# A decoder layer on one core: weights' sums two quarters ahead, and the softmax's scaling moved into the exponential

## The chip, the cores and the metric

The kernel runs on one core of one Trainium2 chip. The metric is the device time of one execution in microseconds (us). A core has five engines that matter here, each with an instruction queue of its own: TensorE (PE in the profile; PEld is its loading of stationary operands), VectorE (DVE), ScalarE (ACT), GpSimd (POOL) and SyncE (SP), which only issues transfers here. An engine takes its instructions in order; an instruction that waits for another engine holds everything behind it in its queue.

## The reference

The input `x` has 32 sequences of 64 tokens with 512 features, all float32. The layer has three stages, each added to its input after a layer norm:

```python
q = rmsnorm(x @ Wq + bq, gq); k = rmsnorm(x @ Wk + bk, gk); v = x @ Wv + bv   # 32 heads of 128
attn = softmax(q @ k.T / sqrt(128)) @ v;  x = x + attn @ Wo + bo
x = x + cross_attention(layernorm(x), ctx)
x = x + top8_of_64_router_mix(layernorm(x))
```

Only the first stage is touched. For it two things matter. The norm of a query row is one factor for all its scores, the norm of a key row is one factor for a column of scores. And the softmax is taken over 64 keys for each query.

## The kernel before

**Tiling.** There are 2048 tokens, cut into two halves of two quads each; a quad is four tiles of 128 tokens (8 sequences). Heads are taken two at a time, a head group `hg` of 0 to 15. The products of inputs with Wq, Wk and Wv are made with Strassen's scheme in Winograd's form, with 7 products in the place of 8; for most head groups in two levels, 49 products in the place of 64. The seven transformed inputs of a half (`inner_x`, from `halves_x`) are kept in seven blocks of a pool of 13 blocks (`blocks`, 2048 floats a partition). The weights need sums too. They are made per head group by `WeightSet`: set 0 to 3 belong to the outer products (1, 5), (2, 6), (7, 3) and (4), and each holds the raw or outer-summed parts (`raw`) and four inner sums (`more`).

**Windows and steps.** Group 0 of each half is done with one level, one quad after the other (`single`). Groups 1 to 15 are done in a window of both quads (`double`, `Window`). A window has four quarters, one for each weight set, and a quarter has four steps; (k, m) means step m of quarter k. `Window.outer` gives the order of products: step 0 has products 1 and 5, step 1 has 6 and 2, step 2 has 7 and 3, step 3 has 4 (in quarter 3, with a single outer product: 1 and 2; 6 and 5; 7 and 3; 4). Products 1, 6, 7 and 4 add onto one and the same PSUM bank `pa`; between two of them a copy (`keep`, L779 or L789, and the L792 of `end`) must have read it. Beside the products each step takes a part of the values' products (`Window.v`, at L978 for `ValueGroup`), of which windows of odd `hg` have none left in quarter 3.

**Attention beside the products.** `Line` carries finished units (a head group of a quad) through attention. In a window, `scale` stands at (1,0) and (2,0), `turn` at (1,1) and (3,2), `attend` at (1,3) and, as `end`, at (3,3). `attend` issues, in this order: the scores of one unit (PE), the mix of the unit before with its values (PE), at the end of a window also the inverse roots of the norms (ACT, L725 and L727, by transfer into DRAM and back by `fetch`, L624), the softmax (`probabilities`, L667) and the store of the mixed unit (`store`, four ACT instructions L710 and a transfer).

**The softmax** (L304 to L318) is a generator. Its first part multiplies scores by `gains` (DVE L309), takes the maximum over 64 keys (L310), subtracts it (L311) and takes the exponential (ACT L312). `gains` holds the keys' inverse roots, broadcast over partitions by `fetch`, times the queries' inverse roots `rq`, multiplied in by POOL in `scale` (L646). Its second part, sums (DVE L315), reciprocals (L317) and the product with them (POOL L318), is put into the list `waiting`. `take_waiting` takes one entry from it. In a window that happens twice a step: after the products of the step (L891), and at the end of `v` (L754), after the values' products. So the second part of a softmax issued at (1,3) or (3,3) is issued in the next step 0, behind that step's copies of products 1 and 5 and ahead of the values' work.

**What sets the order.** In the attention stage the order on PE, DVE, ACT and POOL is that of the program (`manual_schedule`, with `plan` and `behind` as the lists of what goes into which step). SP's transfers are placed by the planner.

**Weights.** `load_qk` (L1748) issues a set's loads and `sums_of` with `inner_sums` its sums on POOL: L175 subtracts outer parts (128x512), L199 inner ones (128x256; 128x128 for the fourth set). In a window's quarter k the set k+2 is loaded at step 0, and the set k+1 is summed at steps 1 and 2 (sets 4 and 5 are the next window's 0 and 1). Each set of queries and keys is loaded from both weights; the fourth takes two outer subtractions. Values' sets are loaded and summed at half that pace.

Of the kernel before, what the change touches and what calls it, by code (L numbers as in the profile page):

```python
# [8 lines left out]
F32 = mybir.dt.float32  # L9
# [32 lines left out]
def decoder_layer(  # L42
# [47 lines left out]
    class Weights:  # L90
# [3 lines left out]
        def __init__(self, name, hg, queues, between=None):  # L94

            parts = []
            self.right = {}
            for n, pair in enumerate(((1, 7), (2, 3), (5, 6), (4,))):
                it = block(f"w{n}_{name}")[:, 0 : 4 * W3].rearrange(
                    "p (h c j d) -> p h c j d", h=2, c=2, j=3  # L100
                )
                parts.append(it)
                self.right.update({i: it[:, h] for h, i in enumerate(pair)})
            for k in range(2):
                for j, src in enumerate((wq, wk, wv)):
                    for c in range(2):
                        queues[j].dma_start(
                            out=parts[k][:, :, c, j, :],
                            in_=src[bass.ts(2 * k + c, P), bass.ts(hg, HW)].rearrange(
                                "p (h d) -> p h d", d=HD  # L110
                            ),
                        )
                if between and k == 0:
                    between()
            self.values = {i: it[:, :, 2, :] for i, it in self.right.items()}
# [28 lines left out]
    class WeightSet:  # L144
# [2 lines left out]

        def __init__(self, n, name, sources, width, base):  # L150
            self.n = n
            it = block(f"ws{n}_{name}")
            self.raw = it[:, 0 : 8 * HD].rearrange("p (o c f) -> p o c f", o=2, c=2)
            self.more = it[:, 8 * HD : 16 * HD].rearrange("p (e o d) -> p e o d", e=4, o=2)
            for j, src in enumerate(sources):
                to = self.raw[:, :, :, j * width : (j + 1) * width]
                if n < 2:
                    for c in range(2):
                        nc.sync.dma_start(
                            out=to[:, :, c],  # L160
                            in_=src[bass.ts(2 * n + c, P), base : base + 2 * width].rearrange(
                                "p (o f) -> p o f", o=2
                            ),
                        )
                else:
                    base_ = base + (width if n == 2 else 0)
                    nc.sync.dma_start(
                        out=to.rearrange("p o c f -> p (o c) f"),
                        in_=src[:, base_ : base_ + width].rearrange("(k p) f -> p k f", p=P),
                    )  # L170
            self.slots = slice(1, 2) if n == 3 else slice(0, 2)

        def outer_sums(self, before):
            def subtract(out, a, b):
                nc.gpsimd.tensor_tensor(  # L175
                    *(it.rearrange("p c f -> p (c f)") for it in (out, a, b)), ALU.subtract
                )

            a, b = (self.raw[:, o] for o in range(2))
            if self.n == 0:  # L180
                subtract(b, b, a)
            elif self.n == 1:
                subtract(b, b, before.raw[:, 1])
            elif self.n == 2:
                subtract(a, b, a)
            else:
                subtract(b, b, before.raw[:, 0])
                subtract(b, b, a)

        def inner_sums(self, part):  # L190
            at = self.slots
            b11, b12, b21, b22 = (
                self.raw[:, at, c, j * HD : (j + 1) * HD] for c in range(2) for j in range(2)
            )
            t1, t2, t4, t7 = (self.more[:, e, at, :] for e in range(4))
            for out, a, b in ((t1, b12, b11), (t2, b22, t1), (t4, b21, t2), (t7, b22, b12))[
                2 * part : 2 * part + 2
            ]:
                nc.gpsimd.tensor_tensor(out, a, b, ALU.subtract)  # L199

        def inner(self, s):

            if self.n == 3:
                s = 1
            b11, _, b21, b22 = (
                self.raw[:, s, c, j * HD : (j + 1) * HD] for c in range(2) for j in range(2)
            )
            t1, t2, t4, t7 = (self.more[:, e, s, :] for e in range(4))
            return {1: b11, 2: b21, 3: b22, 4: t4, 5: t1, 6: t2, 7: t7}

    normed = scratch.tile([NT // 2, P, D], F32, tag="normed", name="normed")
# [89 lines left out]
            nc.tensor.transpose(pt[:, j, :], src[:, j, :], ident)  # L301
        return pt

    def softmax(s, gains, prob, name):  # L304


        g, k = s.shape[1], s.shape[2]
        mx = small.tile([P, g], F32, tag="mx", name=f"mx_{name}")
        nc.vector.tensor_tensor(prob, s, gains, ALU.mult)  # L309
        nc.vector.tensor_reduce(mx, prob, AX.X, ALU.max)  # L310
        nc.vector.tensor_tensor(prob, prob, _bc(mx, k), ALU.subtract)  # L311
        nc.scalar.activation(prob, prob, AF.Exp)  # L312
        yield
        sums = small.tile([P, g], F32, tag="sums", name=f"sums_{name}")
        nc.vector.tensor_reduce(sums, prob, AX.X, ALU.add)  # L315
        inv = small.tile([P, g], F32, tag="inv", name=f"inv_{name}")
        nc.vector.reciprocal(inv, sums)  # L317
        nc.gpsimd.tensor_tensor(prob, prob, _bc(inv, k), ALU.mult)  # L318

    quads = {}  # L320
    halves_x = {}
# [118 lines left out]
    class HeadGroup:  # L440
# [7 lines left out]
        def __init__(self, hg, quad, w, kept):  # L448
            self.hg, self.quad, self.w, self.name = hg, quad, w, f"{hg}_{quad}"

            self.qk, self.gains = {}, None
            self.v = {
                (h, ab): kept[:, h, 2 * (hg % 2) + ab, :, :] for h in range(HG) for ab in range(2)
            }
# [169 lines left out]
        def fetch(self):  # L624

            if self.gains is None:
                both = work.tile([P, 2, NQ, P], F32, tag="rsb", name=f"g_{self.name}", bufs=2)
                self.gains = both[:, 0, :, :]  # L630
            self.rq = small.tile([P, NQ * 2], F32, tag="rq", name=f"rq_{self.name}")
            for h in range(HG):
                rows = slice(h * SEQ, (h + 1) * SEQ)
                rq, rk = (self.row[j, h].rearrange("a b p -> (a b p)") for j in range(2))
                nc.sync.dma_start(
                    out=self.gains[rows].rearrange("p i k -> p (i k)"),
                    in_=rk.partition_broadcast(SEQ),
                )
                nc.sync.dma_start(
                    out=self.rq[rows], in_=rq.rearrange("(g n) -> n g", n=SEQ)  # L640
                )

        def scale(self):

            it = self.gains.rearrange("p i (b k) -> p (i b) k", b=2)
            nc.gpsimd.tensor_tensor(it, it, _bc(self.rq, SEQ), ALU.mult)  # L646
            k = self.all[:, :, 1, :]
            nc.scalar.activation(k, k, AF.Copy, scale=gqk)

# [17 lines left out]
        def probabilities(self):  # L667
            self.prob = work.tile([P, NQ, P], F32, tag="prob", name=f"prob_{self.name}", bufs=1)
            it = softmax(
                self.s.rearrange("p i b k -> p (i b) k"),  # L670
                self.gains.rearrange("p i (b k) -> p (i b) k", b=2),
                self.prob.rearrange("p i (b k) -> p (i b) k", b=2),
                self.name,
            )
            next(it)
            waiting.append(lambda: next(it, None))

        def turn_probabilities(self):

# [53 lines left out]
    class Window:  # L733
# [5 lines left out]
        def __init__(self, units, n, half, values):  # L739
# [6 lines left out]
            both = work.tile([P, 2, NQ, P], F32, tag="rsb", name=f"g_{self.name}", bufs=2)  # L746
            for t, unit in enumerate(units):
                unit.row = self.row[t]
                unit.gains = both[:, t, :, :]

        def v(self):
            if self.values:
# [994 lines left out]

    def load_qk(n, k):  # L1748
        hg, half = groups[n]
        qk_sets[n, k] = WeightSet(k, f"q{hg}_{half}", (wq, wk), HD, hg * HW)  # L1750

    def load_v(half, g, k):
        v_sets[half, g, k] = WeightSet(k, f"v{g}_{half}", (wv,), HW, g * 2 * HW)

    def sums_of(sets, *at):

        it = sets[at]
        it.outer_sums(sets.get((*at[:-1], at[-1] - 1)))
        it.inner_sums(0)

    for n, (hg, half) in enumerate(groups):
# [53 lines left out]
        else:  # L1815
# [2 lines left out]
            def also(n, m, it):  # L1818
                more.setdefault((n, m), []).append(it)

            places = [(n, k) for k in range(4)] + [(n + 1, k) for k in range(2)]
            for k in range(4):
                for at in places[k + 2 if (hg, k) != (1, 0) else 1 : k + 3]:
                    if at[0] == n or hg < NHG - 1:
                        also(k, 0, lambda at=at: load_qk(*at))
                at = places[k + 1]
                if at[0] == n or hg < NHG - 1:
                    also(k, 1, lambda at=at: sums_of(qk_sets, *at))
                    also(k, 2, lambda at=at: qk_sets[at].inner_sums(1))
            for k in range(2):  # L1830
                at = (half, hg // 2, 2 * (hg % 2) + k + 1)
                if at[2] == 4:
# [253 lines left out]
```

## Time and profile before

Three runs took 1883.17, 1883.83 and 1885.5 us; the median is 1883.83. The profiled execution took 1886.6 us, its span (first to last instruction) is 1884.9 us, and its granted TensorE clock 0.995.

| of the profiled execution | value |
|---|---|
| PE busy | 1831.8 us, 97% of the span |
| DVE busy | 1298.2 us, 69% |
| POOL busy | 1170.1 us, 62% |
| ACT busy | 664.9 us, 35% |
| two-level products of queries and keys (L768), busy on PE | 731.9 us |
| inner weight sums for them (L199 on POOL) | 337.1 us, 480 instructions |
| exponential of the softmax (L312 on ACT) | 40.4 us, 64 instructions |
| subtraction of the maximum (L311 on DVE) | 58.0 us, 64 instructions |
| scaling of `gains` (L646 on POOL) | 66.6 us, 60 instructions in windows |

How it is read: a group is all instructions of one line, engine and shape, with its busy time, the mean of one in ns, and the idle time of the engine ahead of them. A wait names the engine and line that released the waiting one last. A timeline row has the start in us, the duration, the engine and line, and in brackets the idle time ahead of it; "x4" means four instructions of one kind merged into one row. Two windows, an even and an odd one, take about 83 us together and repeat seven times in each half.

### The profile page before, as it was taken

How to read it: one execution, taken by the hardware profiler on the slowest of the kernel's cores; microseconds unless marked ns; L12 is line 12 of the kernel's file. 1: busy time of each engine (PE TensorE's matmuls, PEld its weight loads, DVE VectorE, ACT ScalarE, POOL GpSimd, SP SyncE). 2: the span in 40 equal slices, each digit the busy share in tenths (PEclk: the TensorE clock that was granted, in tenths of full speed). 3: DMA queues.
4: the chain of work that ended last, by engine and by line, in shares of the span. 5: the costliest groups of instructions: out<-in, count | busy, mean ns of one | idle time of the engine just before them, and what ended most of it. 6: DMA issues, size and time to landing. Idle time of an engine off the chain costs nothing.

```text
span 1884.9 us, 41677 instructions
## 1 busy us (share of the span) xinstructions
PE 1831.8 (97%) x16500; PEld 1569.0 (83%) x16500; DVE 1298.2 (69%) x2270; ACT 664.9 (35%) x1483; POOL 1170.1 (62%) x1414
## 2 busy tenths in 40 slices
PE   8999999999999989999999999999999999999998
PEld 7887888888888878888888888888888778888876
DVE  6667778787868766677877777787876354544465
ACT  3344443443344433434344433443321212211222
POOL 3678787878888775777888787878833121211120
PEclk9999999999999999999999999999999999999999
DMA  3334444444444443334444344444745222132100
GB/s 114 96 104 134 130 123 121 125 130 116 122 114 114 132 117 90 92 103 124 114 113 125 106 121 113 113 114 118 239 145 191 104 92 79 71 115 101 59 26 23
DMA packets 340241, 211.20 MB, mean 112 GB/s; under 512 B 82320, under 2 KB 319440, under 8 KB 335952
## 3 DMA queue, kind: packets, MB, share of 16 engines
q1 hardware_dynamic: 331856, 202.45, 36.6%
q10 hardware_dynamic: 8192, 6.10, 1.0%
q8 instruction: 131, 2.15, 0.5%
q14 instruction: 62, 0.51, 0.1%
HBM read 168.12 MB, written 40.37 MB: 111 GB/s over the span
## 4 chain that ended last, share of the span: by engine, by line
PE 77%; POOL 11%; DVE 9%; issue 3%; DMA 0%; ACT 0%; POOLq 0%; SPq 0%; DVEq 0%; ACTq 0%
PE p_w L768 24%; PE py L1070 21%; PE va L978 6%; POOL ws_q L175 4%; PE vb L978 4%; PE s L658 4%; POOL qk L848 3%; PE ms_w L904 3%; PE o L695 3%; DVE qk L779 3%; POOL ws_q L199 2%; PE pa L528 2%; POOL g_w L646 2%; PE va L473 1%; PE pt_p L301 1%
## 5 line engine op out<-in xcount | busy, mean ns | idle before, releaser
L768 PE MATMUL p_w<-x,ws_q 128*128 128x256 f32 x2940 | 731.9, 386 | 34.2 <-POOL ws_q L199 20.0
L768 PEld LDWEIGHTS p_w<-x,ws_q 128*128 128x128 f32 x2940 | 521.9, 191 | 113.1 <-POOL ws_q L199 31.3
L199 POOL TENSOR_TENSOR ws_q<-ws_q 128x256 f32<-128x256 f32 x480 | 337.1, 712 | 21.0
L437 ACT ACTIVATE sq<-qk 128x512 f32<-128x512 f32 x256 | 157.5, 629 | 362.6 <-POOL qk L848 219.3
L779 DVE TENSOR_TENSOR qk<-p_w,qk 128x512 f32<-128x512 f32 x360 | 210.6, 596 | 83.6 <-PE p_w L768 72.8
L792 DVE TENSOR_TENSOR qk<-p_w,qk 128x512 f32<-128x512 f32 x360 | 224.0, 624 | 57.7 <-PE p_w L768 49.9
L1070 PE MATMUL py<-wo,a 128*128 128x256 f32 x992 | 227.0, 382 | 0.0
L978 PEld LDWEIGHTS va<-ws_v,x 128*128 128x128 f32 x1568 | 209.0, 191 | 21.0 <-DVE v L994 10.0
L978 PE MATMUL va<-ws_v,x 128*128 128x128 f32 x1568 | 212.6, 276 | 4.4 <-DVE v L994 4.4
L1070 PEld LDWEIGHTS py<-wo,a 128*128 128x128 f32 x992 | 183.8, 190 | 33.5 <-issue 9.0
L318 POOL TENSOR_TENSOR prob<-prob,inv 128x512 f32<-128x512 f32 x64 | 72.3, 1129 | 209.0 <-DVE inv L317 143.0
L978 PEld LDWEIGHTS vb<-ws_v,x 128*128 128x128 f32 x1176 | 154.5, 192 | 6.5
L978 PE MATMUL vb<-ws_v,x 128*128 128x128 f32 x1176 | 158.5, 275 | 0.0
L1070 PE MATMUL py<-wo_t,a 128*128 128x256 f32 x672 | 154.9, 381 | 0.0
L199 POOL TENSOR_TENSOR ws_v<-ws_v 128x256 f32<-128x256 f32 (+1 forms) x224 | 147.4, 668 | 8.8
L1201 POOL TENSOR_TENSOR x<-x,p 128x256 f32<-128x256 f32 x42 | 40.7, 991 | 163.8 <-ACT p L1254 72.9
L1070 PEld LDWEIGHTS py<-wo_t,a 128*128 128x128 f32 x672 | 124.7, 190 | 18.9 <-issue 2.4
L175 POOL TENSOR_TENSOR ws_q<-ws_q 128x512 f32<-128x512 f32 x90 | 116.8, 1298 | 2.4
L710 ACT ACTIVATE ot<-o,bvt 128x256 f32<-128x256 f32 x256 | 99.2, 469 | 2.2 <-PE o L695 2.2
L309 DVE TENSOR_TENSOR prob<-s,g_w 128x512 f32<-128x512 f32 x60 | 41.3, 688 | 84.4 <-PE s L658 66.1
L848 POOL TENSOR_TENSOR qk<-qk 128x256 f32<-128x256 f32 x120 | 89.1, 742 | 5.3 <-DVE qk L792 0.6
L312 ACT ACTIVATE prob<-prob 128x512 f32<-128x512 f32 x64 | 40.4, 631 | 135.2 <-DVE prob L311 135.2
(276 smaller groups left out, 2654.9 us busy)
## 6 DMA issues: line engine op xcount, KB each, us to landing
mixed<-ot SPq DMA_DIRECT2D x64, 512.0 KB
a<-mixed SPq DMA_DIRECT2D x32, 1024.0 KB
ws_q<-in_wq_dram SPq DMA_DIRECT2D x120, 128.0 KB
ws_q<-in_wk_dram SPq DMA_DIRECT2D x120, 128.0 KB
ws_q<-in_wq_dram SPq DMA_DIRECT2D x60, 256.0 KB
ws_q<-in_wk_dram SPq DMA_DIRECT2D x60, 256.0 KB
g_w<-row_w SPq DMA_DIRECT2D x120, 128.0 KB
ws_v<-in_wv_dram SPq DMA_DIRECT2D x56, 256.0 KB
```

The costliest lines, as they stand in the source:

```text
L175: nc.gpsimd.tensor_tensor(*(it.rearrange("p c f -> p (c f)") for it in (out, a, b)), ALU.subtract)
L199: nc.gpsimd.tensor_tensor(out, a, b, ALU.subtract)
L318: nc.gpsimd.tensor_tensor(prob, prob, _bc(inv, k), ALU.mult)
L437: nc.scalar.activation(sq, of, AF.Square)
L658: nc.tensor.matmul(s[h * SEQ : (h + 1) * SEQ, i, b, :], qk[:, 0, tok], qk[:, 1, tok], start=True, stop=True,)
L710: nc.scalar.activation(ot[:, h, :, b * SEQ : (b + 1) * SEQ], o[b][:, h, :, :], AF.Identity, bias=bvt[:, hg * HG + h : hg * HG + h + 1],)
L768: nc.tensor.matmul(bank[:, s, :], right[s][i], inner_x[self.half, o][i], start=first and s == 0, stop=True, skip_group_check=True,)
L779: nc.vector.tensor_tensor(to(t, j), bank, add(t, j), ALU.add)
L792: nc.vector.tensor_tensor(to(t, j), bank, to(t, j), ALU.add)
L848: on.tensor_tensor(to, to, what, ALU.add)
L978: nc.tensor.matmul(bank[:, s, bass.ts(t, HD)], x[:, bass.ts(t, HD)], right[s][i], start=first and s == 0 and t == 0, stop=True, skip_group ...
L1070: nc.tensor.matmul(py, a[:, g, :], b[g // KH][:, g % KH, :], start=n == 0 and g == 0, stop=n == last and g == NHG - 1,)
```

## The change

**Softmax.** `gains` becomes `rk`, the keys' inverse roots alone; POOL's multiplication by `rq` goes from `scale`. The maximum is taken over scores times `rk`; a small DVE instruction makes minus the maximum times `rq`, 8 values a partition. The subtraction over 512 columns goes. In the place of one exponential over 512 columns stand eight over 64, one for each of the 8 groups of 64 keys in a partition's row, since scale and bias of an ACT instruction are one value a partition: `rq` is the scale, the small result the bias. Four of them are issued in the first part, then the generator yields; the other four are a second part, and sums, reciprocals and product a third. Two entries go into `waiting` in the place of one.

**Weights' sums.** In quarter k the set k+3 is loaded and the set k+2 is summed, so sums stand two quarters ahead of their products; the first window of a half loads sets 1 to 3 in its first quarter and sums sets 2 and 3 together in its second. Four blocks hold the sets of queries and keys. The fourth set is not loaded: its outer part is the difference of the two outer parts of the second set (`before.raw`), one subtraction. Two of the inner sums (t1 and t7) are made by one instruction of twice the size.

**Layouts.** A set's parts are laid out so that a load's rows are of 256 floats, as they lie in the weights, in place of 128; loads of the two row chunks are joined, those of the third set (and of the values' third and fourth) split by row halves. The one-level weights (`Weights`) are loaded by 6 transfers in place of 12, in the same way.

```diff
-                    "p (h c j d) -> p h c j d", h=2, c=2, j=3
+                    "p (c j h d) -> p c j h d", h=2, c=2, j=3
...
-                self.right.update({i: it[:, h] for h, i in enumerate(pair)})
+                self.right.update({i: it[:, :, :, h, :] for h, i in enumerate(pair)})
...
-                    for c in range(2):
-                        queues[j].dma_start(
-                            out=parts[k][:, :, c, j, :],
...
+                    queues[j].dma_start(
+                        out=parts[k][:, :, j].rearrange("p c h d -> p c (h d)"),
...
-        def __init__(self, n, name, sources, width, base):
-            self.n = n
+        def __init__(self, n, name, sources, base):
+            self.n, self.full = n, n != 3 or len(sources) == 1
             it = block(f"ws{n}_{name}")
...
+            self.slots = slice(1, 2) if n == 3 else slice(0, 2)
+            if not self.full:
+                return
+            width = places[0].shape[-1]
+            for to, src in zip(places, sources):
                 if n < 2:
-                    for c in range(2):
+                    nc.sync.dma_start(
+                        out=to.rearrange("p c o f -> p c (o f)"),
+                        in_=src[bass.ts(n, 2 * P), base : base + 2 * width].rearrange(
+                            "(c p) f -> p c f", p=P
+                        ),
+                    )
+                else:
+                    base_ = base + (width if n == 2 else 0)
+                    for o in range(2):
                         nc.sync.dma_start(
-                            out=to[:, :, c],
...
+                            out=to[:, :, o],
+                            in_=src[bass.ts(o, 2 * P), base_ : base_ + width].rearrange(
...
+            elif self.full:
+                subtract(b, b, before.raw[:, :, :, 0])
+                subtract(b, b, a)
             else:
-                subtract(b, b, before.raw[:, 0])
-                subtract(b, b, a)
+                subtract(b, before.raw[:, :, :, 0], before.raw[:, :, :, 1])
...
-            for out, a, b in ((t1, b12, b11), (t2, b22, t1), (t4, b21, t2), (t7, b22, b12))[
-                2 * part : 2 * part + 2
-            ]:
-                nc.gpsimd.tensor_tensor(out, a, b, ALU.subtract)
+            if part == 0:
+                nc.gpsimd.tensor_tensor(
+                    self.more[:, 0:2, at, :],
+                    self.raw[:, :, 1, at],
+                    self.raw[:, 0, :, at],
+                    ALU.subtract,
+                )
+            else:
+                nc.gpsimd.tensor_tensor(t2, b22, t1, ALU.subtract)
+                nc.gpsimd.tensor_tensor(t4, b21, t2, ALU.subtract)
...
-    def softmax(s, gains, prob, name):
+    def softmax(s, rk, rq, prob, name):
...
-        nc.vector.tensor_tensor(prob, s, gains, ALU.mult)
+        neg = small.tile([P, g], F32, tag="neg8", name=f"neg_{name}")
+        nc.vector.tensor_tensor(prob, s, rk, ALU.mult)
         nc.vector.tensor_reduce(mx, prob, AX.X, ALU.max)
-        nc.vector.tensor_tensor(prob, prob, _bc(mx, k), ALU.subtract)
-        nc.scalar.activation(prob, prob, AF.Exp)
+        nc.vector.scalar_tensor_tensor(neg, mx, -1.0, rq, ALU.mult, ALU.mult)
+
+        def exps(part):
+            for c in range(part * g // 2, (part + 1) * g // 2):
+                at = slice(c, c + 1)
+                nc.scalar.activation(
+                    prob[:, c, :], prob[:, c, :], AF.Exp, bias=neg[:, at], scale=rq[:, at]
+                )
+
+        exps(0)
+        yield
+        exps(1)
         yield
         sums = small.tile([P, g], F32, tag="sums", name=f"sums_{name}")
...
-            it = self.gains.rearrange("p i (b k) -> p (i b) k", b=2)
-            nc.gpsimd.tensor_tensor(it, it, _bc(self.rq, SEQ), ALU.mult)
             k = self.all[:, :, 1, :]
...
-            waiting.append(lambda: next(it, None))
+            waiting.extend([lambda: next(it, None)] * 2)
...
-        it.outer_sums(sets.get((*at[:-1], at[-1] - 1)))
+        before = at[-1] - (1 if it.full else 2)
+        it.outer_sums(sets.get((*at[:-1], before)))
...
-            places = [(n, k) for k in range(4)] + [(n + 1, k) for k in range(2)]
+            places = [(n, k) for k in range(4)] + [(n + 1, k) for k in range(3)]
+            makes = [places[k + 2 : k + 3] for k in range(4)]
+            loads = [places[k + 3 : k + 4] for k in range(4)]
+            if hg == 1:
+                loads[0] = places[1:4]
+                makes[0], makes[1] = places[1:2], places[2:4]
             for k in range(4):
-                for at in places[k + 2 if (hg, k) != (1, 0) else 1 : k + 3]:
+                for at in loads[k]:
                     if at[0] == n or hg < NHG - 1:
                         also(k, 0, lambda at=at: load_qk(*at))
-                at = places[k + 1]
-                if at[0] == n or hg < NHG - 1:
-                    also(k, 1, lambda at=at: sums_of(qk_sets, *at))
-                    also(k, 2, lambda at=at: qk_sets[at].inner_sums(1))
+                for at in makes[k]:
+                    if at[0] == n or hg < NHG - 1:
+                        also(k, 1, lambda at=at: sums_of(qk_sets, *at))
+                        also(k, 2, lambda at=at: qk_sets[at].inner_sums(1))
```

## The prediction

> **What bounds the kernel now.** I read the busy shares first, then who waits for whom, then the timelines of two neighbouring windows, engine by engine, and last the groups by shape for durations.
>
> ```profile
> span 1884.9 us, 41677 instructions
> PE 1831.8 (97%) x16500; PEld 1569.0 (83%) x16500; DVE 1298.2 (69%) x2270; ACT 664.9 (35%) x1483; POOL 1170.1 (62%) x1414
> ...
> PE p_w L768 <- POOL ws_q L199: 20.0, 28, 1.3
> PE p_w L768 <- DVE qk L779: 6.7, 19, 0.6
> ```
>
> TensorE (PE) is busy 97% of the span, so every gain must come out of about 53 us of idle time, and every new wait of PE is paid in full. The largest wait is for GpSimd (POOL) making weight sums: 28 times, always the same two places in 14 of the odd windows. The timeline of PE there (start, duration, group, wait ahead of it), quarter 3 of the window at 648 to 685:
>
> ```profile
> 679.56 1.13 PE L768 MATMUL p_w<-x,ws_q 128*128 128x256 f32 x4
> 680.87 1.13 PE L768 MATMUL p_w<-x,ws_q 128*128 128x256 f32 x4 [0.18 <-POOL ws_q L199]
> 683.25 1.13 PE L768 MATMUL p_w<-x,ws_q 128*128 128x256 f32 x4 [1.25 <-POOL ws_q L199]
> ```
>
> Four of these matmuls take 0.87 us when they follow each other (eight take 1.73 in the chain), so the step at 680.87 starts 0.44 late, and the one at 683.25 starts 1.51 late. Step (3,0) at 679.56 is 0.36 late too (0.87 + 0.44 behind the steps before it), for the outer sum of L175. That is 2.3 us a window, and all of it is the fourth set, whose sums stand only one quarter ahead. Even windows lose 0.2 at (3,0).
>
> Now the place where the softmax sits. Window start at 647.58, the same window: ScalarE (ACT), then VectorE (DVE), then PE.
>
> ```profile
> 649.21 0.63 ACT L312 ACTIVATE prob<-prob 128x512 f32<-128x512 f32 x1 [1.88 <-DVE prob L311]
> 649.74 1.55 ACT L710 ACTIVATE ot<-o,bvt 128x256 f32<-128x256 f32 x4
> 651.17 0.86 ACT L782 ACTIVATE qk<-p_w,bqd 128x256 f32<-128x256 f32 x2
> ```
> ```profile
> 648.05 1.12 DVE L311 TENSOR_TENSOR prob<-prob,mx 128x512 f32<-128x512 f32 x1
> 649.10 0.68 DVE L789 TENSOR_TENSOR qk<-p_w,bqd 128x512 f32<-128x512 f32 x1
> 649.87 0.69 DVE L315 TENSOR_REDUCE sums<-prob 128x8 f32<-128x512 f32 x1
> 650.59 0.20 DVE L317 RECIPROCAL inv<-sums 128x8 f32<-128x8 f32 x1
> 650.71 0.64 DVE L991 TENSOR_TENSOR v<-va,v 128x512 f32<-128x512 f32 x1
> 651.37 0.69 DVE L789 TENSOR_TENSOR qk<-p_w,bqd 128x512 f32<-128x512 f32 x1
> ```
> ```profile
> 652.92 1.89 PE L768 MATMUL p_w<-x,ws_q 128*128 128x256 f32 x8
> ```
>
> To be seen: the row sum L315 starts 0.03 us after the exponential ends (649.84), and DVE works strictly in the order of the program. Behind it stands L789 at 651.37, which reads the bank `pa` after product 6; product 7, PE's group at 652.92, adds onto that bank and may not start before. L789 ends at 652.06, and where PE does wait for such a copy (663.43 behind a copy ending at 663.29) it starts 0.14 after it: 0.72 us of slack here.
>
> **The exponential, now eight.** Before, one instruction of 0.63, whose successor starts 0.53 after it. The prices of the new ones come from these groups (mean ns last before the bar):
>
> ```profile
> L437 ACT ACTIVATE sq<-qk 128x512 f32<-128x512 f32 x256 | 157.5, 629 | 362.6 <-POOL qk L848 219.3 <-DVE qk L792 59.5 <-DVE qk L779 53.1
> L648 ACT ACTIVATE qk<-qk,gqk 128x1024 f32<-128x1024 f32 x64 | 73.8, 1153 | 0.0
> L1424 ACT ACTIVATE ex_f<-lg_f,neg_f 128x64 f32<-128x64 f32 x14 | 4.8, 340 | 21.6 <-DVE neg_f L1421 21.6
> L1662 ACT COPY bqk<-pt_b 128x64 f32<-128x64 f32 x1 | 0.2, 231 | 0.0
> ```
>
> 64 columns with a per-partition bias take 0.34 (L1424), 0.11 over the copy without one (0.231). No row has scale and bias both per partition. Copies from PSUM grow from 0.369 at 256 columns to 0.582 at 512, 0.83 ns a column; by that L437 at 1024 would be 1.055, and L648 with its per-partition scale takes 1.153: 0.10 more. So 0.34 + 0.10 = 0.44, and as successors start about 0.10 before the end (four L710 of 0.469 in 1.55), 0.34 each in a row. Bounds: 0.17 if neither operand cost anything (0.26 less the overlap), 0.43 if nothing overlapped. I take 0.34.
>
> The nearest row has one such operand and stands at 0.24 in a row; by it alone the total would be 1933 (worked out below). The Trainium skill, "ScalarE: Activation LUTs", section "What ACT_TABLE_LOAD costs", gives 186 ns + 0.833 a column, about 93 for each per-partition operand and about 93 of overlap; for 64 columns an estimate of 0.33 in a row, so it speaks against eight short ones, and by it the sum below is some 4 us lower.
>
> **The wait that this makes.** Half of the exponentials are issued in the attend step, then come the four L710, and the other half one list entry later, at the head of the next step, behind its two L782. L315 follows at the second entry. DVE loses L311 and gains a 128x8 instruction (0.20, as L317; at most 0.69 as the reductions). At the window start above: negated maximum 648.05 to 648.25; exponentials from 648.29, 4 x 0.34 to 649.65; L710 1.42 to 651.07; L782 0.73 to 651.80; second half 3 x 0.34 + 0.44 to 653.26. L315 653.30, L317 654.02, L789 654.14 to 654.82, product 7 at 654.96 in place of 652.92: **2.04 us**. The other three places by the same steps:
>
> - Even window start (605.98; negation from 606.45, product 7 before at 611.32): second half ends 611.65, L789 612.53 to 613.21, product 7 at 613.35: 2.03.
> - Even window, attend at (1,3) (negation from 627.66, product 7 before at 632.47, no L782): second half ends 632.14, copy L779 633.02 to 633.70, product 7 at 633.84: 1.37, less the 0.2 at (3,0): 1.17.
> - Odd window, (1,3) (negation from 670.43, product 7 before at 674.73): product 7 at 676.61, 1.88. Then quarter 3. Followed through DVE's queue, which now runs 1.9 late with little idle time in it: L994 680.24, the copy for (3,1) ends 682.65, (3,1) at 682.79, its copy 683.55 to 683.95, (3,2) at 684.09 instead of 683.25. So 0.84 is left: the 2.3 us that POOL gives back are mostly eaten, since the copies of DVE bind almost as early as POOL did (before, the copy ahead of (3,1) ended at 680.71, 0.16 ahead of PE).
>
> Queued behind the wait on DVE are the copies and the value sums; on ACT, L648 and the value copies shift by 1 to 2 us, and the next users are over 2 us later; POOL's L318 comes 2.3 to 3.3 later, and its product is turned a quarter later (620.94 for the softmax at 605).
>
> **The sums two quarters ahead.** A set's sums get a quarter (some 10 us) more lead, so the waits for L199 and L175 go: gains of 2.3 and 0.2, already netted above. POOL loses per window two L646 (1.11 each), one L175 (1.27) of the fourth set, and joins two L199 (0.78 each) into one of 128x512: between 1.27 (L175) and 1.56, I take 1.3. Some 4.5 us of POOL a window, all off the path once PE no longer waits for it. What would be late next are L848's additions at (2,2), which DVE and the squares wait for: odd window, POOL frees L318 at 676.9, L848 to 678.4, sums 2.65, L848 681.0 to 682.6, ahead of the 683.5 where DVE needs them.
>
> **Loads.** SP issues 8 instead of 12 loads a window for queries and keys (2, 2, 4, 0), at 0.4 to 0.5 each, and 2 x 256 KB less for each fourth set; values stay at 6, the first weights go from 12 to 6. They are hidden: a load is issued a quarter ahead of its sum, as before, and now two quarters and more ahead of its use. The ring of four leaves no spare block (7 inputs + 4 + 2 value sets = 13), so a load waits for PE to finish the set three quarters back, as SP does now (199 us for p_w at L167). If that cover failed, the sums would still have a quarter: bounds 0 and the old 2.3 a window; I take 0.
>
> **The sum.** 14 odd windows x (2.04 + 0.84) = 40.3; 14 even x (2.03 + 1.17) = 44.8; the two first windows, without the POOL waits of the others, 2 x (2.04 + 1.88) = 7.8; the second unit of each half's single pair, an estimate of 1 each (between 0 and 2.04): 2; the tail, where PE already waits 0.46 for L318 at 1377.84 and the probabilities come between 1.2 and 2.9 later: 2. Together +97. The profiled execution took 1886.6, 2.8 over the median: 1983.6, or 1981 on the median's scale.
>
> **Rivals.**
> - Cheaper exponentials: each 0.01 less in a row takes 0.08 off each place. At 0.24 the places give 1.24, 0.04, 1.23, 0.37: 14 x 2.88 + 9 = +49, 1933. At 0.17: 0.68, -0.5, 0.67, -0.2: about +14, 1898. At 0.43: +142, 2026. L648 speaks against the first two.
> - Faster: L315 doesn't hold DVE's copies. One mechanism: the row sums of the second half reach DVE's queue behind the copy of product 6, so PE never waits; then only the POOL waits go. Gain between 20.7 (the waits of PE as listed) and 14 x 2.3 + 14 x 0.2 = 35: 1849 to 1863. It decides if the sums are issued at least 2.0 us later in DVE's queue or the eight exponentials cost under 0.08 each. The order L789, L315, L317, L991 in the profile, which is the program's, speaks against it.
> - POOL stays the wait: if the fused sums or the full ring made the sets late again, the 2.3 would stay on top of the rest: 1981 + 14 x 1.5, about 2002. POOL's 4.5 us less speaks against it.
>
> **How the numbers follow.** As forecast, 1960 to 2000: 0.60; cheaper exponentials, 1890 to 1960: 0.22; faster: 0.10; above 2000: 0.06; within 0.2% (what a measurement of this kernel can tell from no change, some 4 us): 0.02. The range, 1898 to 2005, leaves out the faster case and the far end.
>
> **What would show it.** Right: PE's longest waits for p_w turn from POOL L199 to DVE's copies, at steps (0,2) and (2,2), 1 to 2 us each, twice a window; the row sums wait for ACT's exponentials 60 times; no wait for L199. ACT's busy time grows by some 140 us. Wrong: if the exponentials stand 0.2 apart, or DVE takes its copies ahead of the row sums, or PE's order leaves more slack at product 7 than 0.15 to 0.9 us.

## The result and the profile after

The changed kernel takes 2003.55 us (median of 4 runs, 2001.9 to 2007.45) against 1883.96 us for the kernel before on the same chip (4 runs, 1883.17 to 1885.5): a ratio of 1.0637, 95% interval 1.0618 to 1.0655. It is 119.6 us slower; 97 were forecast. The profiled execution has a span of 2002.6 us, 117.7 more than the one before, at a mean granted clock of 0.990.

The head of the page after, with the busy shares:

```profile
span 2002.6 us, 41393 instructions
PE 1853.2 (93%) x16500; PEld 1577.0 (79%) x16500; DVE 1278.3 (64%) x2270; ACT 803.0 (40%) x1931; POOL 1022.9 (51%) x1144
```

The waits of TensorE (PE) after, in us, times, longest:

```profile
PE p_w L791 <- DVE qk L802: 68.5, 100, 2.3
PE p_w L791 <- DVE qk L812: 50.0, 29, 1.9
PE pt_p L314 <- POOL prob L342: 6.3, 2, 3.5
```

GpSimd (POOL) has 147 us less to do, and no wait of PE for a weight sum is left (20.0 us before). In its place PE waits 118.5 us for VectorE's (DVE's) copies of the products (L802 and L812 are L779 and L789 of before). ScalarE (ACT) has 138 us more. The groups that say why; the last number behind the bar is the wait ahead of the group:

```profile
L330 ACT ACTIVATE prob<-prob,neg,rq 128x64 f32<-128x64 f32 x512 | 183.6, 436 | 91.4 <-DVE neg L325 91.4
L339 DVE TENSOR_REDUCE sums<-prob 128x8 f32<-128x512 f32 x64 | 43.9, 686 | 155.1 <-ACT prob L330 155.1
L871 DVE TENSOR_TENSOR qk<-qk 128x256 f32<-128x256 f32 x120 | 101.4, 845 | 0.0
```

The row sums wait 155.1 us for the exponentials, where they waited 1.5. And VectorE's additions of the two quadrants (L871, L848 of before) take 845 ns each; no instruction of theirs was changed. The same group before:

```profile
L848 DVE TENSOR_TENSOR qk<-qk 128x256 f32<-128x256 f32 x120 | 70.5, 587 | 0.0
```

The start of an even window after, on ACT, then on DVE, then PE (the window starts at 645.93, its product 7 at 653.26):

```profile
646.78 1.44 ACT L330 ACTIVATE prob<-prob,neg,rq 128x64 f32<-128x64 f32 x4 [1.12 <-DVE neg L325]
648.12 1.53 ACT L733 ACTIVATE ot<-o,bvt 128x256 f32<-128x256 f32 x4
649.54 0.83 ACT L805 ACTIVATE qk<-p_w,bqd 128x256 f32<-128x256 f32 x2
650.26 1.44 ACT L330 ACTIVATE prob<-prob,neg,rq 128x64 f32<-128x64 f32 x4
```
```profile
651.73 0.69 DVE L339 TENSOR_REDUCE sums<-prob 128x8 f32<-128x512 f32 x1 [3.94 <-ACT prob L330]
652.45 0.20 DVE L341 RECIPROCAL inv<-sums 128x8 f32<-128x8 f32 x1
652.57 0.64 DVE L812 TENSOR_TENSOR qk<-p_w,bqd 128x512 f32<-128x512 f32 x1
```
```profile
653.26 3.32 PE L791 MATMUL p_w<-x,ws_q 128*128 128x256 f32 x8 [1.83 <-DVE qk L812]
```

This is the chain that the prediction drew, link by link: four exponentials of 0.436 each in 1.44 us, the stores, the two biased copies, the other four exponentials, then the row sum with the copy of product 6 behind it, then PE 0.05 us after that copy (0.14 had been put down). DVE stands still for 3.94 us.

### The profile page after: what moved, and what is told of

It is laid out like the page before. It is cut to its first block, busy times and chain, and to the rows that moved or that the text cites. A ratio compares the mean times of both kernels' runs of the same rounds, so it can differ in the third digit from the quotient of the medians.

```text
span 2002.6 us, 41393 instructions
## 1 busy us (share of the span) xinstructions
PE 1853.2 (93%) x16500; PEld 1577.0 (79%) x16500; DVE 1278.3 (64%) x2270; ACT 803.0 (40%) x1931; POOL 1022.9 (51%) x1144
## 4 chain that ended last, share of the span: by engine, by line
PE 60%; DVE 21%; ACT 13%; issue 3%; DMA 1%; POOL 1%; SPq 0%; DVEq 0%; ACTq 0%; POOLq 0%
PE py L1093 19%; PE p_w L791 18%; ACT prob L330 8%; PE va L1001 4%; ACT ot L733 4%; DVE qk L802 4%; PE s L680 3%; PE ms_w L927 3%; DVE sums L339 2%; DVE mx L324 2%; DVE qk L871 2%; DVE prob L323 2%; PE vb L1001 2%; DVE qk L815 2%; DVE v L1017 1%
## 5 line engine op out<-in xcount | busy, mean ns | idle before, releaser
L791 PE MATMUL p_w<-x,ws_q 128*128 128x256 f32 x2940 | 747.2, 391 | 128.3 <-DVE qk L802 68.5
L791 PEld LDWEIGHTS p_w<-x,ws_q 128*128 128x128 f32 x2940 | 527.4, 192 | 220.5 <-DVE qk L802 94.2
L802 DVE TENSOR_TENSOR qk<-p_w,qk 128x512 f32<-128x512 f32 x360 | 210.3, 592 | 84.5 <-PE p_w L791 82.4
L330 ACT ACTIVATE prob<-prob,neg,rq 128x64 f32<-128x64 f32 x512 | 183.6, 436 | 91.4 <-DVE neg L325 91.4
L206 POOL TENSOR_TENSOR ws_q<-ws_q 128x512 f32<-128x512 f32 x120 | 139.2, 1160 | 9.4
L339 DVE TENSOR_REDUCE sums<-prob 128x8 f32<-128x512 f32 x64 | 43.9, 686 | 155.1 <-ACT prob L330 155.1
L186 POOL TENSOR_TENSOR ws_q<-ws_q 128x512 f32<-128x512 f32 x90 | 114.5, 1272 | 2.3 <-PE p_w L791 2.3
L871 DVE TENSOR_TENSOR qk<-qk 128x256 f32<-128x256 f32 x120 | 101.4, 845 | 0.0
```

Of the source, the lines that this page charges most:

```text
L206: nc.gpsimd.tensor_tensor(self.more[:, 0:2, at, :], self.raw[:, :, 1, at], self.raw[:, 0, :, at], ALU.subtract,)
L330: nc.scalar.activation(prob[:, c, :], prob[:, c, :], AF.Exp, bias=neg[:, at], scale=rq[:, at])
L791: nc.tensor.matmul(bank[:, s, :], right[s][i], inner_x[self.half, o][i], start=first and s == 0, stop=True, skip_group_check=True,)
L802: nc.vector.tensor_tensor(to(t, j), bank, add(t, j), ALU.add)
L871: on.tensor_tensor(to, to, what, ALU.add)
```

## Experiments

**Each half of the change alone.** The first kernel is the changed one with the softmax of before; weights' sums and layouts stay changed. The second is the kernel before with the new softmax.

```diff
-        nc.vector.scalar_tensor_tensor(neg, mx, -1.0, rq, ALU.mult, ALU.mult)
...
+        nc.vector.tensor_tensor(prob, prob, _bc(mx, k), ALU.subtract)
+        nc.scalar.activation(prob, prob, AF.Exp)
...
-            waiting.extend([lambda: next(it, None)] * 2)
+            waiting.append(lambda: next(it, None))
```

> The weights' part alone: sums two quarters ahead, ring of four, fourth set from the second, new layouts and loads; the softmax as before the change. Wait theory (the loss is DVE's copies standing behind row sums that wait for the second half of the exponentials): PE's waits for L199 go, at (3,2) of odd windows PE starts 1.0 earlier (its next limit is DVE's copy), even windows gain 0 to 0.2, so some 17 us are gained: 1855 to 1880. Rival (the ring without a spare block, the split loads or the changed sums cost the time): slower than before, up to 2000.

> The softmax part alone, weights as before the change. Wait theory: product 7 is late by 2.0, 2.0, 1.4 and about 1.5 us in the four places of a pair of windows, and POOL's waits for the fourth set shrink as PE itself comes later: 1985 to 2020, the same as the whole change within 20 us. Rival (the time is lost in the weights' part): within 20 us of the kernel before.

Weights' sums alone: 1881.09 us, ratio 0.9982 (0.9973 to 0.9992): a gain of 3 to 4 us, below what was expected of it. The softmax alone: 2037.15 us, ratio 1.0813 (1.0795 to 1.0831), above what was expected. So the whole loss is the softmax's, and the two halves don't add: 152 lost and 4 gained would give some 2032, not 2004. With the old sums PE also keeps its wait for POOL (17.3 us), and the granted clock falls to 0.980, where the changed kernel has 0.990.

Weights' sums alone, waits of PE and the additions:

```profile
PE p_w L781 <- DVE qk L792: 25.0, 74, 0.8
L861 DVE TENSOR_TENSOR qk<-qk 128x256 f32<-128x256 f32 x120 | 103.9, 865 | 0.0
```

POOL's 20 us of waits went as expected, and 25.0 us behind DVE's copies stand where 6.7 did. The additions got 278 ns longer with the old softmax too, so that belongs to the weights' part of the change and not to the softmax's.

**Without the wait in the middle.** The first kernel issues all eight exponentials ahead of the stores, as one part; the second keeps the two parts and puts the row sums one place later in the list, behind the copies that they held up.

```diff
         exps(0)
-        yield
         exps(1)
...
-            waiting.extend([lambda: next(it, None)] * 2)
+            waiting.append(lambda: next(it, None))
```
```diff
-            waiting.extend([lambda: next(it, None)] * 2)
+            waiting.extend([lambda: next(it, None), lambda: None, lambda: next(it, None)])
```

> The whole change, but all eight exponentials are issued in the first part, ahead of the four stores' copies, and the row sums again one entry later. ACT does the same work in another order. Wait theory: the row sums' wait ends after 8 x 0.34 instead of 8 x 0.34 + 1.42 (+ 0.73 at a window's start), so product 7 is late by 0.5 at an odd window's start, 0 at an even one's, 0.5 at (1,3) of even windows and about 1.2 in odd ones; PE's pauses stay under 1.3 us and its clock stays granted: 1895 to 1925. Rival (ACT's 140 us more of work are the price, wherever they stand): 1990 to 2010.

> The whole change, with an empty entry between the second half of the exponentials and the row sums, so that the sums are issued at step (0,1) or (2,1), behind that step's copy of product 6. Same instructions on every engine. Wait theory: product 7 no longer waits for the row sums, PE's waits of 1 to 2 us for the copies go and the clock stays granted; what is left is the tail of quarter 3, where DVE's additions are slower beside POOL: 1865 to 1895. Rival (ACT's work or the weights' part is the price): 1985 to 2010.

All eight ahead of the stores: 1919.78 us, ratio 1.0185 (1.017 to 1.02), as expected; the row sums' wait falls from 155.1 to 95.6 us. Row sums one place later: 1905.1 us, ratio 1.0108 (1.0093 to 1.0123). That one empty entry, with not an instruction more or less, takes back 98 of the 120 us:

```profile
PE p_w L791 <- DVE qk L802: 28.1, 70, 0.8
L871 DVE TENSOR_TENSOR qk<-qk 128x256 f32<-128x256 f32 x120 | 110.0, 917 | 0.0
L339 DVE TENSOR_REDUCE sums<-prob 128x8 f32<-128x512 f32 x64 | 43.8, 684 | 30.7 <-ACT prob L330 30.7
```

So the wait that cost the time is the row sums' on DVE, ahead of the copy of product 6. It missed its range by 10 us, and the additions, now 917 ns, show where to look.

**What makes the exponential dear.** The eight exponentials lose their two per-partition operands, and nothing else changes.

```diff
                 nc.scalar.activation(
-                    prob[:, c, :], prob[:, c, :], AF.Exp, bias=neg[:, at], scale=rq[:, at]
+                    prob[:, c, :], prob[:, c, :], AF.Exp, scale=0.001
                 )
```

> The changed kernel, with its eight 128x64 exponentials at a fixed scale and without a bias: it leaves out the queries' inverse roots and the row maximum, so the softmax's numbers are others, but the count of instructions, their order and the queue stay. If the two per-partition operands are what makes one exponential take 0.335 us to the next, the four of a half fall from 1.44 us to some 0.7, both halves' row sums come 0.7 to 1.4 us earlier in each place, and the time falls to 1905 to 1930. If the price is the count of instructions, the four still take over 1.2 us and the time stays at 1980 to 2005.

1893.01 us, ratio 1.0041 (1.0026 to 1.0056), 12 us under the expected 1905 to 1930 and far from the other theory's 1980 to 2005. Its ACT queue at a window's start:

```profile
561.88 0.69 ACT L329 ACTIVATE prob<-prob 128x64 f32<-128x64 f32 x4 [0.72 <-DVE mx L324]
562.48 1.55 ACT L732 ACTIVATE ot<-o,bvt 128x256 f32<-128x256 f32 x4
563.90 0.85 ACT L804 ACTIVATE qk<-p_w,bqd 128x256 f32<-128x256 f32 x2
564.62 0.71 ACT L329 ACTIVATE prob<-prob 128x64 f32<-128x64 f32 x4
```

Four take 0.69 to 0.71 us, 256 ns each, so they follow each other in 0.145 us in place of (1.44 - 0.436)/3 = 0.335. The two operands together cost 0.19 us an instruction; which of them costs how much wasn't tested. They also start some 0.2 us sooner, since they don't need the negated maximum. With 16 instructions in 2 places a window these two things are what 110 of the 120 us hang on. The count of instructions is not: with 512 instructions on ACT in place of 64 the kernel is 12 us behind the weights' part alone (1881.09). The prediction's rival for 0.17 us had given 1898.

**The additions beside POOL.** With the softmax of before, the weights' sums of quarters 2 and 3 go to steps (1,3) and (3,3), away from the additions; in the second kernel the values' sums are moved too, by the second diff.

```diff
-                        also(k, 1, lambda at=at: sums_of(qk_sets, *at))
-                        also(k, 2, lambda at=at: qk_sets[at].inner_sums(1))
+                        first, then = ((k, 1), (k, 2)) if k < 2 else ((2 * k - 3, 3),) * 2
+                        also(*first, lambda at=at: sums_of(qk_sets, *at))
+                        also(*then, lambda at=at: qk_sets[at].inner_sums(1))
```
```diff
+                    first, then = ((0, 3), (1, 1)) if k == 0 else ((3, 1), (3, 2))
+                    also(*first, lambda at=at: sums_of(v_sets, *at))
+                    also(*then, lambda at=at: v_sets[at].inner_sums(1))
```

> The weights' part alone, but the query and key sums of quarters 2 and 3 stand at (1,3) and (3,3), behind the attention work, instead of at (2,1), (2,2), (3,1), (3,2). Same instructions. Port theory (DVE's additions of (2,2) to (3,1), both operands in SBUF, stand still while a POOL instruction runs, which is what took the gain of the earlier sums): their mean falls from 865 ns to 550 to 700, PE's 25 us of waits for DVE's copies fall to 8 to 15: 1862 to 1876. Rival (DVE's copies in quarter 3 are simply too many for the shorter quarter): waits and time as in the weights' part alone, 1878 to 1884.

> As the one before, and the values' sums of (2,3) and (3,1) moved to (3,1) and (3,2). Port theory: DVE's additions near 500 ns, a further 3 to 8 us: 1856 to 1872, unless the values' sums now come too late for the next window. Rival: as the one before within 2 us.

1857.19 us, ratio 0.9856 (0.9841 to 0.987), and 1857.77, ratio 0.9859 (0.9843 to 0.9876), better than expected and alike: the values' sums didn't matter (additions of 588 ns, where some 500 were expected). The place alone is worth 24 us, and the additions are back at their old time:

```profile
L861 DVE TENSOR_TENSOR qk<-qk 128x256 f32<-128x256 f32 x120 | 70.4, 587 | 0.0
```

One part of the expectation failed: PE's waits behind the copies L792 were to fall to 8 to 15 us and stay at 25.0. What fell are its waits behind the copies L805 (6.1 to 0.4), for the values (5.7 to nothing) and for POOL's transformed inputs at L439 (4.5 to 0.7), and its busy time by 9.6. Nor is all of the 24 us due to the additions: 18 of it lie in the 28 windows behind the first ones, some 7 in the two first windows and at the change of halves, where the waits at L439 and two drops of the granted clock are gone.

**Is the lead of two quarters worth anything?** The old softmax again and the fourth set from the second, but sums one quarter ahead and loads two.

```diff
-            makes = [places[k + 2 : k + 3] for k in range(4)]
-            loads = [places[k + 3 : k + 4] for k in range(4)]
+            makes = [places[k + 1 : k + 2] for k in range(4)]
+            loads = [places[k + 2 : k + 3] for k in range(4)]
```

> The weights' part, but sums one quarter ahead and loads two, as before the change; the fourth set from the second, the joined inner sums and the new layouts stay. Tells more lead from less work. If the lead is what takes PE's waits for the sums away, they stay at 8 us or more. If the smaller work of the fourth set is enough (1.3 us less at (2,1), 0.4 less at (2,2)), the waits for POOL's sums are under 4 us and the time is within 4 us of the weights' part alone, 1877 to 1885.

1864.69 us, ratio 0.9894 (0.9879 to 0.9908): 16 us better than the lead of two quarters as it was placed, though PE waits for the sums again:

```profile
PE p_w L781 <- DVE qk L792: 14.3, 31, 1.0
PE p_w L781 <- POOL ws_q L213: 9.6, 14, 0.7
```

Neither theory had this outcome. The smaller work takes half of the 20 us of waits for POOL by itself. The lead takes the other half, and more comes back behind DVE's copies, with additions of 865 ns in place of 667. In its better place the lead is worth 7.5 us (1857.19 against 1864.69).

**The changed kernel with its sums moved.** The same edit as above, with the new softmax in place.

> The changed kernel with one edit: the sums of the queries and keys for quarters 2 and 3 of the list are made at steps (1,3) and (3,3), and no longer beside quarter 3's additions of 128x256 on VectorE. If those additions, slowed by GpSimd beside them (845 ns in place of 587), cost the changed kernel the 0.63 us of each odd and the 0.98 us of each even window that quarter 3 lost, the time falls by about 14 x 1.6, to 1978 to 1985, and the additions go back to some 590 ns. If quarter 3 was late because of what the softmax did before it, the additions get faster and the time stays above 1995.

1986.39 us (1981.86 to 1991.96), ratio 1.0536 (1.0518 to 1.0554): 17 us are gone, where 19 to 26 were expected, and the additions are at 651 ns, where some 590 were. Its windows (each from the `attend` that closes the window before, 4.1 us ahead of its own first product): start and end in us, length, PE busy with its count, granted clock, DMA share and GB/s:

```profile
635.13:680.23 45.10, 41.99 (x444) 1.00 0.31 83
...
1050.89:1095.70 44.81, 39.65 (x415) 1.00 0.39 106
...
1325.22:1372.49 47.27, 41.55 (x416) 0.96 0.36 102
```

An even window of before takes 41.67 and an odd one 41.64 (below), so the even one loses 3.43 and the odd one 3.17, where the prediction had 3.20 and 2.88. In the changed kernel an even window at full clock loses 4.15, and this odd one 3.89 (45.53). The odd windows at a clock of 0.96, of which there are 9 among 28, lose another 1.9 to 2.7 each: some 20 us, against some 9 in the changed kernel (shown below). The difference is more than the step by which the time lies above its range.

**Both stalls taken away.** The new softmax with its row sums one place later, and the sums moved.

> The changed kernel with the row sums' entry one place later (as in sums_later) and with the sums of the queries and keys that lay in quarter 3 moved away from its additions (as in sums_moved). sums_moved took 1857. If the softmax part has something to give once neither the row sums nor the additions stand in the way (it saves POOL and VectorE work), this is below 1855. If the exponentials still hold ScalarE's copies and stores, it stays above sums_moved, at 1865 to 1890: the split costs more than the two multiplications that it saves, wherever its entries stand.

1869.88 us, ratio 0.9915 (0.9898 to 0.9932): faster than before, and still 12.7 us behind the same kernel with the old softmax (1857.19). The multiplication saved on POOL and the subtraction saved on DVE buy nothing that PE waits for. The profiled spans differ by 14.1, of which 8.6 lie behind the last window (526.9 us from its end against 518.3), and PE's waits for the probabilities are 5.6 us against 0.5.

## Why the prediction was right or wrong

The sign, the mechanism and its place were right. The total was 23 us short, through two terms that were missing, a tail that was too small and one term that went the other way. So 2003.55 lies 1.5 us under the upper end of the stated range and already in the part, above 2000, that was given a chance of 0.06. That it lies inside is luck in part: without the 6.4 us at the start, which the prediction had put at nothing, it would lie outside.

| step of the prediction | predicted | measured |
|---|---|---|
| exponentials, one to the next | 0.34 us | 0.335 |
| product 7 at the start of an even window | +2.03 | +2.00 (562.19 - 554.85 against 5.34) |
| at the start of an odd window | +2.04 | +1.82 (607.77 - 600.61 against 5.34) |
| place at (1,3), even | +1.37 | +1.30 (29.79 from the start against 26.49, less 2.00) |
| place at (1,3), odd | +1.88 | +1.82 (30.79 against 27.15, less 1.82) |
| odd window, total at step (3,2) | +2.88 | +2.89 (38.56 against 35.67) |
| odd window at full clock, total at its end | +2.88 | **+3.62** (41.22 against 37.60) |
| even window at full clock, total at its end | +3.20 | **+4.16** (41.72 against 37.56) |
| drop of the granted clock | not in the sum | **8 of 28 windows, some 9 us** |
| start, up to the first window | 0 | **-6.4** |
| the two first windows and the start of the second half | +9.8 | +5.3 |
| tail | +2 | +7.2 |

**Right.** The rival in which POOL stays the wait falls: no sum of weights is waited for, and that its figure of 2002 comes nearest is chance. The price of the exponential, on which the first rival hung, was worked out from rows with one operand (the one with a bias, L1424, also sums what it writes), and lay 5 ns off. The faster rival named its own condition, the row sums 2.0 us later in DVE's queue; the run that does this is 98 us faster than the change and yet not faster than before. Only with the additions out of the way as well does it come to 1869.88, near the 1849 to 1863 of that rival, with the help of the 6.4 us at the start that the rival didn't count.

The Trainium skill comes as close: "ScalarE: Activation LUTs", section "What ACT_TABLE_LOAD costs", gives, as estimates from its figures, some 0.33 us with two per-partition operands and 186 + 53 - 93 = 146 ns with none. The runs show 0.335 and 0.145.

**Wrong, first: "What would be late next are L848's additions".** The prediction asked whether POOL's half of the additions comes late. It doesn't. But the sums that now stand two quarters ahead lie in quarter 3 beside DVE's half. Timelines after, quarter 3 of an even window, DVE and then POOL:

```profile
682.17 0.97 DVE L871 TENSOR_TENSOR qk<-qk 128x256 f32<-128x256 f32 x1
...
684.52 0.99 DVE L871 TENSOR_TENSOR qk<-qk 128x256 f32<-128x256 f32 x1
...
686.70 0.41 DVE L871 TENSOR_TENSOR qk<-qk 128x256 f32<-128x256 f32 x1
```
```profile
682.15 1.59 POOL L871 TENSOR_TENSOR qk<-qk 128x256 f32<-128x256 f32 x2
683.70 0.72 POOL L213 TENSOR_TENSOR ws_q<-ws_q 128x256 f32<-128x256 f32 x1
684.50 0.73 POOL L214 TENSOR_TENSOR ws_q<-ws_q 128x256 f32<-128x256 f32 x1
```

The two additions at 682.17 and 684.52 start 0.02 us after a POOL instruction and take 0.97 and 0.99: the second ends at 685.51, 0.28 after POOL's at 684.50 has ended. The one at 686.70 starts between two POOL instructions and takes 0.41. So it is throughout: of the 120 additions 102 start while a POOL instruction runs and end 0.28 us after it has ended (the median; 0.28 to 0.37 for all of them), and the other 18 take 0.41. What the sums change is how much of a POOL instruction is left at that time: over 0.3 us for 85 additions, and for 47 before. The same two additions of an even window before:

```profile
637.01 0.41 DVE L848 TENSOR_TENSOR qk<-qk 128x256 f32<-128x256 f32 x1
...
638.80 0.44 DVE L848 TENSOR_TENSOR qk<-qk 128x256 f32<-128x256 f32 x1
```

DVE had, as the prediction put it, "little idle time" there, so each such half microsecond can reach PE. This would make +0.86 of an even window's quarter 3 where a gain of 0.2 stood, and 0.73 at the end of an odd one: 14 x (1.06 + 0.73) = 25 us. The experiment that moves the sums bears out 0.72 a window, some 20 of these 25: without them the windows at full clock stand at +3.43 and +3.17.

**Wrong, second: a pause was priced at its length.** Windows before, then after, same columns as above:

```profile
601.87:643.54 41.67, 41.61 (x443) 1.00 0.37 103
643.54:685.18 41.64, 39.52 (x415) 1.00 0.46 128
```
```profile
550.75:596.57 45.82, 42.26 (x443) 1.00 0.30 82
596.57:641.83 45.26, 39.84 (x415) 1.00 0.37 106
641.83:689.32 47.49, 43.93 (x443) 0.96 0.29 79
```

Two even windows with the same work and the same pause differ by 1.67 us. The 3.41 us behind product 7's pause in each, after:

```profile
562.19:565.60 3.41, 3.41 (x20) 1.00 0.58 97
653.26:656.67 3.41, 3.41 (x10) 0.58 0.58 91
```

The pause ahead is 1.83 us in both. Behind the second the clock is granted at 0.58, and PE gets 10 instructions done where it gets 20. Five even windows lose 1.67 each in this way, and three odd ones, where the pause of 2.31 is at (1,3), 0.36: some 9 us.

**Wrong, third: "the first weights go from 12 to 6. They are hidden".** The prediction counted all loads in SP's queue. A part of these is issued from ACT's, ahead of the first layer norm's inverse root (L284 before, L297 after). ACT before, then after:

```profile
6.38 1.11 ACTq L107 DMA_DIRECT2D w<-in_wk_dram  x2
8.64 0.90 ACTq L107 DMA_DIRECT2D w<-in_wv_dram  x2
9.64 0.30 ACT L284 ACTIVATE rs_a<-mv_a,ln_eps 128x2 f32<-128x2 f32 x1 [7.43 <-DMA w<-in_wk_dram]
```
```profile
4.58 0.64 ACTq L106 DMA_DIRECT2D w<-in_wv_dram  x1
5.43 0.30 ACT L297 ACTIVATE rs_a<-mv_a,ln_eps 128x2 f32<-128x2 f32 x1 [3.22 <-DVE mv_a L291]
```

Eight transfers on ACT's queue became four, the root comes 4.2 us earlier, PE's first transposes at 6.60 in place of 10.81, and the first window at 52.21 in place of 58.58. The 2.2 us on top fit the clock: over the 3.41 us from the first transpose on it was granted at 0.50 before and at 1.00 after, with 14 instructions of PE in it before and 21 after. All ten kernels with the new layout begin their first window between 51.65 and 52.77, both without it at 58.50 and 58.58. No run changes these loads alone. So the 3 to 4 us that the weights' part gains by itself are this 6.4, less what its windows lose.

**The tail** was undersized: PE waits 3.51 and 2.77 for the probabilities (1490.04 and 1536.07), where 2 in all was put down from a single wait of 0.46.

Summed over the span: -6.4 at the start, +5.3 for the first windows and the change of halves, +111.6 in the other 28 windows (85.1 predicted), +7.2 behind them, which is 117.7. The 28 would lose 118 if all were as in the table; the first even and the last odd window of each half lose less (0.82 and 3.97; 2.91 and 1.93), and so do the first four odd ones, which took 42.5 before.

## What to carry to other kernels

An instruction that waits for a slow neighbour should stand behind everything on its queue that the critical engine needs; here one empty entry in a list of deferred work was worth 98 us. Work made earlier isn't free because it has slack: look at what runs beside its new place, since a GpSimd instruction can double the time of a VectorE addition next to it. And look at every queue that issues a moved transfer, not only at the one that issues most.

The version to keep is the weights' part with its sums moved away from the additions, and the softmax of before: 1857.19 us, 1.4% faster than the kernel before. Since the start gives 6.4 of its 28 us, the layout is a good part of it.

## What the runs showed of the hardware

**A pause of 1.8 us can halve the clock.** In the changed kernel PE has 47 pauses of 1.2 us or more between 90 and 1530 us. None of the 26 below 1.78 us was followed by a lower clock; 5 of the 12 between 1.83 and 1.86 were, and 6 of the 9 above 2 us. In the changed kernel with its sums moved it was none of 33 below 1.78 and 11 of 15 above 2, in the softmax alone none of 25 up to 1.85 and 22 of 34 above. The lower clock lasted some 3.4 us (0.51 over 653.85 to 657.25). The Trainium skill, "TensorE: Matmul & The Clock Gate", section "What's actually happening", has a window of 3413 ns that runs freely, which agrees with the length and with the same pause being punished or not. By its rule in "HAM oscillation — how this bites in real kernels" a pause matters above some 3.4 us; here 1.83 was enough. Why it was enough wasn't tested.

**VectorE's additions of two SBUF operands wait for GpSimd.** 587 ns in the mean before, 865 with the sums beside them, 587 with the sums elsewhere; an addition that starts while a GpSimd instruction runs ends 0.28 us after it. The Trainium skill, "GPSIMD Engine Reference", section "1. Specifications", says that VectorE instructions with two SBUF inputs contend with GpSimd, which the rows agree with; copies that add a PSUM operand (L792 and L805) take 595 and 622 ns with the sums in quarter 3, and 596 and 621 with the sums elsewhere.

**Two per-partition operands make a short ACT instruction more than twice as long to the next one:** 0.335 us in place of 0.145 at 64 columns.
